# Index loads at the start, thin products in column groups, and the opening of the last stage of a four-layer graph network

## The chip, the cores and the metric

The kernel runs on one core of one Trainium2 chip. The metric is the device time of one launch in microseconds (us). Engines are named as in the profile: PE is TensorE's matmul, PEld its weight load, DVE is VectorE, ACT is ScalarE, POOL is GpSimd, SP is SyncE, which here only issues DMAs.

## The reference

512 nodes with 768 features pass through four layers. Each layer adds three things to the residual stream `x`: a graph network over 8704 directed edges, a linear attention ("mix"), and a feed-forward part. What matters for the change:

- The graph networks need, for each pair of nodes, how many edges of each type run between them, and for the first layer the sum of edge features per target node.
- Layers 1 (RGAT, two convolutions) and 3 (GAT) compute attention coefficients per node and head from thin products: 768 features against 24, 6 or 24 columns.
- The feed-forward parts of layers 0 and 2 are mixtures of 8 experts; a router product (768 by 8) picks one expert for each node.
- The last feed-forward part scores all nodes for 16 experts; each expert takes its 64 best nodes, and a shared expert takes all:

```python
sc = sigmoid(xn @ gate.T)                    # 512 x 16
for e in range(16):                          # expert e takes the 64 nodes of highest sc[:, e]
    h = silu(xn[top] @ Wg[e].T) * (xn[top] @ Wu[e].T)      # hidden width 3072
    out[top] += sc[top, e] * (h @ Wd[e].T)
out += (silu(xn @ Ws_g.T) * (xn @ Ws_u.T)) @ Ws_d.T        # hidden width 1536
```

All numbers are float32 on the outside; the kernel computes most products in float32, and the edge counts and a few exactly split operands in bfloat16.

## The kernel before, in words

The residual `x` stays on chip as four tiles of 128 nodes by 768. `xnT` is a normalized copy with features on partitions: six chunks of 128 features by 512 nodes. Every product accumulates over these six chunks in one PSUM tile of 128 by 512 (`ps`; eight exist). `acc` (L320) issues such a chain, `tr` (L325) a transpose, `copy` (L236, L238) empties PSUM on DVE and ACT by turns, `w` (L244) fetches a weight block of 1152 KB by an SP DMA into a ring of buffers. The engines' instruction orders are fixed when the program is built: a scheduler works through the program in its written order, with priorities, and an instruction waits only by semaphores. POOL, SP and ACT each have a queue of their own for the DMAs that they issue, and an issuing instruction takes its place in the engine's order.

**Start.** `Net.__init__` issues the loads of `x` (L179, 1.5 MB) and of the constant columns (L181) on POOL, then builds constants: identities, ones, iotas on POOL; `sel`, `identb`, `lower` and `number` on DVE. `counts` then loads four index vectors on POOL (L391), casts them (L392), builds edge weights `worth` (L399 to L401) and runs four passes, h and g each 0 and 1. A pass has 34 steps j; in each, DVE makes one-hot rows (`ohd` L465 in the first two passes, three `so` L468), and PE adds six 128x512 bf16 products to six PSUM tiles (L471), which an opening product with ones fills (L462). At the end of a pass the six tiles are copied out, split into digits (L478 to L485), and, in between, edge features of a quarter of the edges are split into three bf16 parts (L416 to L419) and multiplied (L424). The first layernorm and the first mix follow in the written order after the counts.

**Thin products.** The router products of both mixtures and of the last stage (`p[:E]` in `moe`, `p[:NX]` in `ffn3`), and the attention coefficients of `rgat` and the GAT, are chains of six matmuls with 8, 6, 16 or 24 stationary columns and 512 moving ones. The result has its few rows on partitions; four transposes turn it to nodes on partitions.

**Last stage.** `last_two` runs the last attention and the GAT side by side, and after the last projection normalizes the four tiles into `xn`; each is also written to DRAM (`there`, L1531, on ACT's queue). `ffn3` opens a ring of 10 weight buffers, transposes `xn` to `xnT`, computes the scores `sc` (Sigmoid, L1675), and ranks the nodes for each expert: `rank` transposes a broadcast of the scores, so that every node sees all others on its row, and DVE counts, per tile of 128 nodes, the greater ones before, the greater ones after, and equal ones with smaller index (L1687, L1690). `choose` compares ranks with 0..63 and gives a one-hot `oh`. For the first pair of experts `gather` multiplies `xn` by `oh` on PE (48 matmuls); for the seven later pairs `fetch` works out the row numbers and reads the rows from `there` by an indirect DMA of POOL (L1726), and `turn` transposes them. Then 64 steps of one 384-wide slice of two experts follow: `up` (L1794, two 64-column groups side by side), Silu, `down` (L1810). The slices of the shared expert, ranks and fetches of later pairs are spread between the steps by a table (`beside`). SP issues the weight blocks in the order of use, each as soon as its ring buffer is free.

Of the kernel before, what the change touches and what calls it, by code (L numbers as in the profile page):

```python
# [10 lines left out]
F32 = mybir.dt.float32  # L11
# [63 lines left out]

def _layout(i):
# [32 lines left out]
    for f, n, g in (("f0", "L0_ffn", "Ws"), ("f2", "L2_ffn", "Wg")):  # L109
        col(f + "_wg", _thin(i[f"{n}_{g}"]))  # L110
        a[f + "_w1"] = np.stack([_blocks(w)[0, 0] for w in i[n + "_W1"]])
        a[f + "_w2"] = _rows(i[n + "_W2"])
        a[f + "_b2"] = np.ascontiguousarray(i[n + "_b2"])
        col(f + "_b1", _col(i[n + "_b1"]))
# [31 lines left out]
    col("f3_gw", _thin(i["L3_ffn_gate_weight"].T))  # L146
# [18 lines left out]
class Net:  # L165
    def __init__(self, ctx, tc, dram, at, out):
# [11 lines left out]
        self.x = keep.tile([P, NT, D], F32, name="x")  # L178
        nc.gpsimd.dma_start(self.x, dram["x"].rearrange("(t p) d -> p t d", p=P))  # L179
        self.cols = keep.tile([P, dram["cols"].shape[1]], F32, name="cols")  # L180
# [6 lines left out]
        for i in range(3):  # L187
            nc.vector.tensor_copy(self.sel[32 * i : 32 * i + 32, :], self.ident[:32, :32])
        self.bias3 = self.rowp.tile([96, 2, D], BF16, name="bias3", bufs=1)
        nc.gpsimd.memset(self.bias3, 0.0)  # L190
        self.which = 0
        self.ones = keep.tile([P, P], F32, name="ones")
# [12 lines left out]
        nc.vector.tensor_copy(self.identb, self.ident)  # L205
        self.big0 = keep.tile([P, 1], F32, name="big0")
        nc.gpsimd.memset(self.big0, -BIG)
        self.onesb = keep.tile([P, P], BF16, name="onesb")
        nc.gpsimd.memset(self.onesb, 1.0)
# [3 lines left out]
        with tc.tile_pool(name="init", bufs=1) as ip:  # L213
            io = ip.tile([P, P], F32, name="io")
            nc.gpsimd.iota(io, pattern=[[1, P]], base=0, channel_multiplier=0, allow_small_or_imprecise_dtypes=True)
            nc.vector.tensor_scalar(self.lower, io, self.me, None, OP.is_gt)

        self.number = keep.tile([P, NT, 2], BF16, name="number")
        nc.vector.tensor_copy(self.number[:, :, 0], self.me.to_broadcast([P, NT]))
        for t in range(NT):  # L220
            nc.gpsimd.memset(self.number[:, t, 1:2], float(t * P))

# [95 lines left out]
    def acc(self, out, pairs):  # L318
        for n, (a, b) in enumerate(pairs):
            self.nc.tensor.matmul(out, a, b, start=n == 0, stop=n == len(pairs) - 1)  # L320
# [6 lines left out]
    def to_fm(self, x, out):  # L327

        ps = [self.ps() for _ in range(KC)]
# [22 lines left out]
    def norm1(self, x, out, t):  # L352
# [8 lines left out]
        nc.scalar.activation(r, mv[:, 1:2], AF.Sqrt, bias=self.eps)  # L361
# [9 lines left out]
    def counts(self, c0, g0):  # L371
# [10 lines left out]
        with ExitStack() as c:  # L382
# [7 lines left out]
            for n, a in enumerate(("src", "dst", "edge_type_3", "edge_type_4")):  # L390
                nc.gpsimd.dma_start(raw[:, n, :], d[a].rearrange("(p j) -> p j", p=P))  # L391
# [10 lines left out]
            io = one.tile([P, N], I16, name="io")  # L402
            nc.gpsimd.iota(io, pattern=[[1, N]], base=0, channel_multiplier=0)
# [6 lines left out]
            def features(q):  # L410
# [7 lines left out]
                nc.scalar.copy(part[:, 1], ea)  # L418
# [38 lines left out]
            for h in range(2):  # L457
                digit = {}
                for g in range(2):
# [3 lines left out]
                    for j in range(g * HJ, (g + 1) * HJ):  # L463
# [3 lines left out]
                        for n in range(3):  # L467
                            nc.vector.tensor_scalar(so[:, n, :], io[:, h * 256 : (h + 1) * 256], ind[:, 0, j : j + 1],  # L468
# [4 lines left out]
                    for (t, n), p in acc.items():  # L473
# [12 lines left out]
                        if g == 1:  # L486
                            finish(h, t, n, lo, hi, *digit[t, n])

                    for q in range((2 * h + g) * EJ // 8, (2 * h + g + 1) * EJ // 8):
                        features(q)  # L490
# [199 lines left out]
    def moe(self, f, act, xn, bs=None):  # L690
# [5 lines left out]
        with ExitStack() as c:  # L696
            one = c.enter_context(tc.tile_pool(name=f + "_one", bufs=1))
            two = c.enter_context(tc.tile_pool(name=f + "_two", bufs=2))
            xnT = one.tile([P, KC, N], F32, name="xnT")
# [8 lines left out]
            wg = self.col(f + "_wg", 0, KC * E).rearrange("p (k e) -> p k e", k=KC)  # L708
            p = self.ps()
            self.acc(p[:E], [(wg[:, k, :], xs[k]) for k in range(KC)])  # L710
            loT = one.tile([E, N], F32, name="loT")
            if bs is None:
                nc.vector.tensor_copy(loT, p[:E])
            else:
                nc.vector.tensor_scalar(loT, p[:E], self.col(bs, 0, 1, E), None, OP.add)
            p = self.ps()
            for t in range(NT):
                self.tr(p[:, t * E : (t + 1) * E], loT[:, t * P : (t + 1) * P])
            lo = one.tile([P, NT, E], F32, name="lo")
            nc.vector.tensor_copy(lo, p[:, : NT * E].rearrange("p (t e) -> p t e", t=NT))  # L720
# [423 lines left out]
    def fold(self, wq, l, H):  # L1144
# [19 lines left out]
        def turn(V, vt):  # L1164
            for a in range(2):
# [3 lines left out]
                nc.scalar.copy(V[:, 3 * a : 3 * a + 3],  # L1169
# [4 lines left out]
    def rgat(self, xT, l, H, V, C, done, between=None):  # L1174
# [4 lines left out]
        with ExitStack() as c:  # L1179
# [6 lines left out]
            qkT = one.tile([J, N], F32, name="qkT")  # L1186
# [8 lines left out]
            p = self.ps()  # L1195
            self.acc(p[:J], [(V[:, k].rearrange("p r h -> p (r h)"), xT[:, k, :]) for k in range(KC)])
            nc.scalar.copy(qkT, p[:J])
# [4 lines left out]
            def side():  # L1202
                p = self.ps()
                for t in range(NT):
                    self.tr(p[:, t * J : (t + 1) * J], qkT[:, t * P : (t + 1) * P])
                nc.scalar.copy(qk.rearrange("p t r h -> p (t r h)"), p[:, : NT * J])
                self.parts(qk3, qkT, qkT, mid, self.copies, nc.vector.tensor_sub)
# [60 lines left out]
    def gnn1(self, V1, xnT):  # L1268
        nc, tc, d = self.nc, self.tc, self.d
        with ExitStack() as c:  # L1270
# [34 lines left out]
            V2 = one.tile([P, KC, 3, 2], F32, name="V2")  # L1305
# [163 lines left out]
    def last_two(self, xn, xnT, out):  # L1469
# [5 lines left out]
        with ExitStack() as c:  # L1475
# [42 lines left out]
            for t in range(NT):  # L1518
# [8 lines left out]
                if over:  # L1527
                    while len(ready) <= t:
                        u = len(ready)
                        self.norm1(self.x, out, u)  # L1530
                        nc.scalar.dma_start(there[u * P : (u + 1) * P, :], out[:, u, :])  # L1531
# [4 lines left out]
    def fold3(self, one):  # L1536
# [7 lines left out]
        V = one.tile([P, KC, 2 * H], F32, name="V")  # L1544
# [10 lines left out]
    def gnn3(self, c, xnT, V):  # L1555
# [19 lines left out]
        qkT = one.tile([2 * H, N], F32, name="qkT")  # L1575
# [5 lines left out]
        p = self.ps()  # L1581
        self.acc(p[: 2 * H], [(V[:, k, :], xnT[:, k, :]) for k in range(KC)])
        nc.scalar.copy(qkT, p[: 2 * H])
        for t in range(NT):
# [7 lines left out]
            if t == 0:  # L1592
                q = self.ps()
                for u in range(NT):
                    self.tr(q[:, u * 2 * H : (u + 1) * 2 * H], qkT[:, u * P : (u + 1) * P])
                nc.scalar.copy(qk.rearrange("p t r h -> p (t r h)"), q[:, : NT * 2 * H])
                self.parts(qk3, qkT, qkT, mid, self.copies, nc.vector.tensor_sub)
# [42 lines left out]
    def ffn3(self, xn, xnT, there):  # L1640
# [5 lines left out]
        with ExitStack() as c:  # L1646
            one = c.enter_context(tc.tile_pool(name="f3_one", bufs=1))
            two = c.enter_context(tc.tile_pool(name="f3_two", bufs=2))
# [3 lines left out]
            self.wp = c.enter_context(tc.tile_pool(name="f3_w", bufs=10, side="right"))  # L1652

            first = self.small.tile([P, 1], F32, name="r3")
            nc.scalar.activation(first, self.eps, AF.Sigmoid)
            io = one.tile([P, P], F32, name="io")
            nc.gpsimd.iota(io, pattern=[[1, P]], base=0, channel_multiplier=0, allow_small_or_imprecise_dtypes=True)
            number = one.tile([P, NT, 2], F32, name="number")
            nc.gpsimd.tensor_copy(number, self.number)
# [5 lines left out]
            self.to_fm(xn, xnT)  # L1665
            gw = self.col("f3_gw", 0, KC * NX).rearrange("p (k e) -> p k e", k=KC)
            p = self.ps()
            self.acc(p[:NX], [(gw[:, k, :], xnT[:, k, :]) for k in range(KC)])
            loT = one.tile([NX, N], F32, name="loT")
            nc.vector.tensor_copy(loT, p[:NX])  # L1670
            p = self.ps()
            for t in range(NT):
                self.tr(p[:, t * NX : (t + 1) * NX], loT[:, t * P : (t + 1) * P])
            sc = one.tile([P, NT, NX], F32, name="sc")
            nc.scalar.activation(sc, p[:, : NT * NX].rearrange("p (t e) -> p t e", t=NT), AF.Sigmoid)  # L1675

            def rank(e):
# [4 lines left out]
                for t in range(NT):  # L1682
                    s = sc[:, t, e : e + 1]
                    for n, (a, b, op) in enumerate(((0, t * P, OP.is_ge), (t * P, N, OP.is_gt))):
                        if a < b:
                            junk = one.tile([P, N], F32, name="junk")
# [263 lines left out]
```

## Time and profile before

| what | before |
|---|---|
| time, median of 3 runs | 4281.39 us (4278.18 to 4281.85) |
| time of the profiled execution | 4283.03 us |
| its span, first to last instruction | 4281.2 us |
| mean granted clock of TensorE | 0.988 |
| PE / DVE / ACT / POOL busy | 4117.0 / 1299.7 / 659.5 / 268.9 us |
| moved by DMA | 710.30 MB |
| weight blocks by SP, last stage (Wg, Wu, Wd) | 3 x 128 of 1152 KB |

The span is cut into windows and slices; the busy time of an engine in a window says how full it was, "GB/s" what the DMA moved. PE runs nearly everywhere; its matmuls are pipelined, so that one row's duration (some 0.6 us) is longer than the distance of two starts (0.43 us for a float32 pass of 512 columns; each float32 matmul shows as two passes).

### The profile page before, as it was taken

The numbers are of one execution on the slowest core, as the hardware profiler recorded it, in microseconds if no ns is written. First come the engines' busy times: TensorE is split into PE (matmuls) and PEld (weight loads), VectorE is DVE, ScalarE is ACT, GpSimd is POOL, SyncE is SP. The second block draws the span as 40 slices with busy tenths as digits, with TensorE's granted clock in tenths as the row PEclk, the third lists the DMA queues.
The fourth block names the chain that finished last, engine by engine and source line by source line (L and its number), as shares of the span: only waits on it lengthen the run. The fifth ranks groups of instructions, "written<-read, shape, count | busy, mean of one in ns | idle before, by whom it ended". The sixth has DMA issues, their size and how long they took to land. (4 is left out here: it accounts for less than half of the span.)

```text
span 4281.2 us, 40171 instructions
## 1 busy us (share of the span) xinstructions
PE 4117.0 (96%) x16392; PEld 2100.7 (49%) x16392; DVE 1299.7 (30%) x3120; ACT 659.5 (15%) x1241; POOL 268.9 (6%) x316
## 2 busy tenths in 40 slices
PE   7989999999989999999999999989999999999998
PEld 3434555554445566755644444445654444444443
DVE  7772111112432125513220101035841122122211
ACT  2121200001312223411200000022610000000000
POOL 1120000001022010000000000021100000000000
PEclk9999999999999999999999999989999999999999
DMA  3111011111047112211201111063079999999998
GB/s 111 52 61 57 23 45 66 67 56 53 18 169 293 38 60 72 107 45 55 106 34 67 45 55 56 0 261 136 1 288 420 419 420 420 420 417 420 419 421 363
DMA packets 98955, 710.30 MB, mean 166 GB/s; under 512 B 12032, under 2 KB 12096, under 8 KB 29392
## 3 DMA queue, kind: packets, MB, share of 16 engines
q1 hardware_dynamic: 77776, 601.13, 35.3%
q0 software_dynamic: 16512, 93.97, 5.8%
q10 hardware_dynamic: 4480, 12.58, 0.8%
q8 instruction: 132, 2.16, 0.2%
q14 instruction: 55, 0.45, 0.0%
HBM read 685.09 MB, written 22.54 MB: 165 GB/s over the span
## 5 line engine op out<-in xcount | busy, mean ns | idle before, releaser
L1794 PE MATMUL ps<-w,xg 128*64 128x384 f32 x3072 | 566.0, 489 | 5.0 <-DMA w<-in_f_Wg_dram 3.0
L1794 PEld LDWEIGHTS ps<-w,xg 128*64 128x64 f32 x3072 | 234.1, 137 | 297.2 <-issue 271.0
L1427 PE MATMUL ps<-aT,w 128*128 128x512 f32 x864 | 372.3, 592 | 0.0
L1810 PE MATMUL ps<-w,hT 128*64 128x384 f32 x1536 | 321.0, 490 | 6.3 <-ACT hT L238 2.5
L320 PE MATMUL ps<-xnT,w 128*128 128x512 f32 (+1 forms) x732 | 320.3, 594 | 0.3 <-ACT xnT L238 0.2
L1427 PEld LDWEIGHTS ps<-aT,w 128*128 128x128 f32 x864 | 164.2, 190 | 203.6 <-issue 202.3
L320 PE MATMUL ps<-w,xnT 128*128 128x384 f32 x672 | 221.6, 486 | 0.2 <-DVE xnT L236 0.2
L320 PEld LDWEIGHTS ps<-xnT,w 128*128 128x128 f32 (+1 forms) x732 | 133.7, 184 | 174.7 <-issue 171.3
L1810 PEld LDWEIGHTS ps<-w,hT 128*64 128x64 f32 x1536 | 132.1, 136 | 169.1 <-issue 143.9
L368 DVE TENSOR_TENSOR x<-x,ps 128x384 f32<-128x384 f32 x224 | 123.4, 553 | 295.0 <-PE ps L320 223.6
L320 PE MATMUL ps<-C,parts 128*128 128x512 bf16 x864 | 189.8, 381 | 4.0 <-DVE inv L1449 4.0
L320 PE MATMUL ps<-w,hT 128*128 128x384 f32 x552 | 184.7, 490 | 3.9 <-ACTq L895 3.9
L471 PE MATMUL ps<-ohd,so 128*128 128x512 bf16 x816 | 181.9, 383 | 2.8 <-DVE so L468 2.8
L320 PEld LDWEIGHTS ps<-w,xnT 128*128 128x128 f32 x672 | 127.0, 190 | 88.6 <-issue 4.7
L1437 DVE TENSOR_TENSOR aT<-inv,ps 128x512 f32<-128x512 f32 x72 | 49.5, 688 | 367.2 <-PE ps L320 367.2
L1797 ACT ACTIVATE h<-ps 128x384 f32<-128x384 f32 x64 | 31.4, 491 | 794.8 <-PE ps L1794 794.8
L1798 DVE TENSOR_TENSOR h<-h,ps 128x384 f32<-128x384 f32 x64 | 35.5, 554 | 377.6 <-PE ps L1794 377.6
L320 PEld LDWEIGHTS ps<-w,hT 128*128 128x128 f32 x552 | 103.1, 190 | 81.4 <-ACT xbT L238 7.6
L320 PE MATMUL ps<-w,aT 128*128 128x384 f32 (+1 forms) x416 | 139.6, 486 | 0.5 <-DVE aT L236 0.4
L320 PEld LDWEIGHTS <-parts 128*128 128x128 bf16 x864 | 84.9, 98 | 110.0 <-issue 11.0
L320 PE MATMUL ps<-xnT,sw 128*128 128x512 f32 x288 | 138.3, 611 | 0.0
L468 DVE TENSOR_SCALAR so<-io,ind,worth 128x256 bf16<-128x256 int16 x408 | 121.7, 355 | 35.5 <-PE ps L471 35.4
(499 smaller groups left out, 4804.4 us busy)
## 6 DMA issues: line engine op xcount, KB each, us to landing
w<-in_f_Wg_dram SPq DMA_DIRECT2D x128, 1152.0 KB, 14.5
w<-in_f_Wu_dram SPq DMA_DIRECT2D x128, 1152.0 KB, 15.2
w<-in_f_Wd_dram SPq DMA_DIRECT2D x128, 1152.0 KB, 16.0
w<-in_g_w_dram SPq DMA_DIRECT2D x54, 1152.0 KB, 5.1
w<-in_m_wqkv_dram SPq DMA_DIRECT2D x24, 1152.0 KB, 6.6
w<-in_g_t_dram SPq DMA_DIRECT2D x12, 1152.0 KB, 5.8
w<-in_m_wp_dram SPq DMA_DIRECT2D x8, 1152.0 KB, 5.3
ea<-in_edge_attr_dram SPq DMA_DIRECT2D x34, 256.0 KB, 2.7
```

The lines of the kernel that those rows point to most:

```text
L320: self.nc.tensor.matmul(out, a, b, start=n == 0, stop=n == len(pairs) - 1)
L368: self.nc.vector.tensor_add(xs, xs, p)
L468: nc.vector.tensor_scalar(so[:, n, :], io[:, h * 256 : (h + 1) * 256], ind[:, 0, j : j + 1], worth[:, n, j : j + 1], OP.is_equal, OP.mult)
L471: nc.tensor.matmul(p, so[:, n, t * P : (t + 1) * P], ohd[:, j, :], start=False, stop=j == (g + 1) * HJ - 1)
L1427: nc.tensor.matmul(outs[nb * 3 + f], w[:, k, f * P : (f + 1) * P], xT[:, k, :], start=first and k == 0, stop=last and k == KC - 1)
L1437: nc.vector.tensor_mul(aT[:, f, :], inv[:, r, :], p)
L1794: nc.tensor.matmul(p[a * 64 : a * 64 + 64, :HW], xg[:, k, a * CAP : (a + 1) * CAP], ws[b][a][:, k, :], start=k == 0, stop=k == KC - 1)
L1797: nc.scalar.activation(h, pg[:, :HW], AF.Silu)
L1798: nc.vector.tensor_mul(h, h, pu[:, :HW])
L1810: nc.tensor.matmul(po[nb][a * 64 : a * 64 + 64, :HW], hT[:, f * P + a * 64 : f * P + a * 64 + 64], wd[a][:, f, nb * HW : (nb + 1) * HW], s ...
```

## The change

Three things are edited. **Start:** the index loads move from POOL's queue to those of SP and ACT, ahead of everything else there; `onesb` and the iota become POOL's first work; DVE's constants go to a function `constants`, which together with the first layernorm is issued after the last `so` (and the last feature part) of the third pass; the first pass's features are issued after the third `so`. **Narrow groups:** `narrow` computes the thin products with weights padded to 32 columns, chunk k in columns 32*(k%4), so that the PSUM tile holds four partial sums; these are added by products with `fours`, four identities of 32 on top of each other (`narrow_tm` gives nodes on partitions; in `rgat` and the GAT a further product gives heads on partitions). The router weights get loads of their own. **Last stage:** `to_fm` can copy the first three node tiles before the last is there, `xn` is given up after it and its room taken by a ring of 13 weight buffers, `there` is written from POOL's queue, Sigmoid's table is called for after the last square root, the first two ranks are computed half by ACT's Sign with a sum, half by a DVE compare with a sum, and the first pair's nodes are fetched from DRAM as the others are, with a second product of the shared expert put between.

The order on each engine in the new program: DVE begins with the cast of the indices; SP with two index loads, then the edge features; ACT with the other two. In the ranks, Sign and the DVE compare of one tile alternate on the two engines, each waiting for the other's read of the shared PSUM tile.

```diff
+        self.onesb = keep.tile([P, P], BF16, name="onesb")
+        nc.gpsimd.memset(self.onesb, 1.0)
+        self.io = keep.tile([P, N], I16, name="io")
+        nc.gpsimd.iota(self.io, pattern=[[1, N]], base=0, channel_multiplier=0)
         nc.gpsimd.dma_start(self.x, dram["x"].rearrange("(t p) d -> p t d", p=P))
...
+        self.fours = keep.tile([P, 32], F32, name="fours")
+        for i in range(4):
+            nc.gpsimd.tensor_copy(self.fours[32 * i : 32 * i + 32, :], self.ident[32 * i : 32 * i + 32, 32 * i : 32 * i + 32])
...
+    def constants(self):
+        nc = self.nc
+        for i in range(3):
+            nc.vector.tensor_copy(self.sel[32 * i : 32 * i + 32, :], self.ident[:32, :32])
+        nc.vector.tensor_copy(self.identb, self.ident)
+        nc.vector.tensor_scalar(self.lower, self.io[:, :P], self.me, None, OP.is_gt)
+        nc.vector.tensor_copy(self.number[:, :, 0], self.me.to_broadcast([P, NT]))
...
+    def narrow(self, w, xs):
+        p = self.ps()
+        for k in range(KC):
+            g = 32 * (k % 4)
+            self.nc.tensor.matmul(p[g : g + 32], w[:, k, :], xs[k], start=k < 4, stop=k + 4 >= KC)
+        return p
+
+    def narrow_tm(self, four, n):
+        p = self.ps()
+        for t in range(NT):
+            self.acc(p[:, t * n : (t + 1) * n], [(four[:, t * P : (t + 1) * P], self.fours[:, :n])])
+        return p[:, : NT * n].rearrange("p (t n) -> p t n", t=NT)
...
-                nc.gpsimd.dma_start(raw[:, n, :], d[a].rearrange("(p j) -> p j", p=P))
+                (nc.sync, nc.scalar)[n % 2].dma_start(raw[:, n, :], d[a].rearrange("(p j) -> p j", p=P))
...
+                    if h == 1 and g == 0:
+                        self.begun = made["so"].ins, made["part"].ins
                     for q in range((2 * h + g) * EJ // 8, (2 * h + g + 1) * EJ // 8):
-                        features(q)
+                        if h == g == 0:
+                            with tc.issue_after(made["third"]):
+                                features(q)
+                        else:
+                            features(q)
...
-                net.norm(net.x, xn)
+                with tc.issue_after(net.begun[0]), tc.issue_after(net.begun[1]):
+                    net.constants()
+                    net.norm(net.x, xn)
...
+            wg = one.tile([P, KC, 32], F32, name="wg")
+            nc.scalar.dma_start(wg.rearrange("p k e -> p (k e)"), d[f + "_wg"])
...
-            self.acc(p[:E], [(wg[:, k, :], xs[k]) for k in range(KC)])
-            loT = one.tile([E, N], F32, name="loT")
+            p = self.narrow(wg, xs)
+            loT = one.tile([P, N], F32, name="loT")
...
-            for t in range(NT):
-                self.tr(p[:, t * E : (t + 1) * E], loT[:, t * P : (t + 1) * P])
-            nc.vector.tensor_copy(lo, p[:, : NT * E].rearrange("p (t e) -> p t e", t=NT))
+            nc.vector.tensor_copy(lo, self.narrow_tm(loT, E))
...
+                self.acc(p[:J], [(self.fours[:, :J], qkT)])
+                nc.scalar.copy(qk.rearrange("p t r h -> p t (r h)"), self.narrow_tm(qkT, J))
+                self.parts(qk3, p[:J], qkT[:J], mid, self.copies, nc.vector.tensor_sub)
...
-                        nc.scalar.dma_start(there[u * P : (u + 1) * P, :], out[:, u, :])
+                        nc.gpsimd.dma_start(there[u * P : (u + 1) * P, :], out[:, u, :])
...
-            self.wp = c.enter_context(tc.tile_pool(name="f3_w", bufs=10, side="right"))
+            self.wp = c.enter_context(tc.tile_pool(name="f3_w", bufs=13))
...
+            side = one.tile([P, 7 * P], BF16, name="side")
+            nc.gpsimd.memset(side[:, : 3 * P], 0.5)
+            nc.gpsimd.memset(side[:, 4 * P :], -0.5)
+            nc.gpsimd.tensor_scalar(side[:, 3 * P : 4 * P], before, -0.5, None, OP.add)
...
+            BIGGER = 2.0 ** 60
+            nc.vector.tensor_scalar(low, sc[:, :, :2], -BIGGER, None, OP.mult)
...
+            def first_rank(e):
+                p = self.ps()
+                for t in range(NT):
+                    self.tr(p[:, t * P : (t + 1) * P], sc[:, t, e : e + 1].to_broadcast([P, P]))
+                for t in range(NT):
+                    junk = one.tile([P, N], BF16, name="sign")
+                    i = nc.scalar.activation(junk, p, AF.Sign, scale=BIGGER, bias=low[:, t, e : e + 1],
+                                             accum_out=signs[:, t, e : e + 1])
+                    junk = one.tile([P, N], BF16, name="junk")
+                    nc.vector.scalar_tensor_tensor(junk, p, sc[:, t, e : e + 1], side[:, (3 - t) * P : (7 - t) * P],
+                                                   OP.is_equal, OP.mult, accum_out=sides[:, t, e : e + 1])
+                return i
...
-            rest = pieces[1:]
+            rest = pieces[2:]
...
             for e in range(2):
-                rank(e)
-            shared(0, 0)
+                last = first_rank(e)
+            nc.vector.tensor_scalar(signs, signs, 0.5, float(N // 2), OP.mult, OP.add)
+            nc.vector.tensor_add(above[:, :, :2], signs, sides)
+            with tc.issue_after(last.ins):
+                last = shared(0, 0)
             choose(0)
-            gather(0)
+            with tc.issue_after(last.ins):
+                last = fetch(0)
+            with tc.issue_after(last.ins):
+                shared(0, 1)
+            turn(0)
             held = up(*steps[0], up_w(*steps[0]))
```

`oh`, `junk` and `number` are bf16 now, and the tiles `rows` and `os` have one buffer each in place of two.

## The prediction

> **What bounds the kernel now.** I read the page's rows in slices first, then the table of windows, then the waits of TensorE (PE), then the timeline where these disagree. TensorE is busy 96% of the span, so a microsecond counts only where it empties TensorE, or where something else is the limit.
>
> ```profile
> PE 4117.0 (96%) x16392; PEld 2100.7 (49%) x16392; DVE 1299.7 (30%) x3120; ACT 659.5 (15%) x1241; POOL 268.9 (6%) x316
> PE   7989999999989999999999999989999999999998
> GB/s 111 52 61 57 23 45 66 67 56 53 18 169 293 38 60 72 107 45 55 106 34 67 45 55 56 0 261 136 1 288 420 419 420 420 420 417 420 419 421 363
> ```
>
> Two ends show themselves: the first slice is only 7 tenths full, and from slice 30 on (3200 us) the DMA stands at 420 GB/s without a gap. The windows of the last stage (time, then PE, PE's weight loads, DVE, ACT, POOL, then clock, DMA share, GB/s) say which is the limit there:
>
> ```profile
> 3140.00:3150.00 10.00, 7.50 (x26) 2.88 (x25) 2.62 (x8) 2.11 (x4) 0.00 (x0) 0.94 1.02 418
> 3160.00:3170.00 10.00, 9.41 (x58) 8.61 (x60) 2.26 (x7) 0.48 (x1) 0.00 (x0) 0.71 0.78 323
> 3170.00:3180.00 10.00, 10.00 (x54) 4.51 (x51) 3.13 (x12) 0.49 (x1) 0.00 (x0) 1.00 0.64 238
> 3180.00:3190.00 10.00, 10.00 (x54) 4.10 (x52) 3.26 (x14) 0.49 (x1) 0.55 (x1) 1.00 0.90 363
> 3500.00:3700.00 200.00, 199.38 (x990) 87.93 (x987) 38.17 (x100) 11.61 (x23) 4.79 (x8) 1.00 1.01 420
> ```
>
> In 3500 to 3700 PE looks full, but its up-products (L1794) sum to 566.0 us over 64 groups, where one undisturbed group took 7.96: 64 x 7.96 = 509. The 57 us between are matmuls held inside a group by weights. So the weight stream sets the end of the last stage. Its only losses are the dips at 3160 to 3190, and its start.
>
> The start is the longest wait of TensorE (us in total, times, longest), and the timeline tells its cause (start, duration, and in brackets the idle time before and its releaser):
>
> ```profile
> PE ps L424 <- DVE ohd L465: 17.1, 1, 17.1
> 5.99 0.57 POOL L391 DMA_DIRECT2D so<-in_src_dram  x1
> 16.43 1.48 DVE L359 BATCH_NORM_STATS2 st<-x 128x6 f32<-128x384 f32 x3 [9.39 <-DMA x<-in_x_dram]
> 24.34 0.27 DVE L392 CAST ind<-so 128x272 f32<-128x272 int32 x1
> 26.42 1.06 PE L471 MATMUL ps<-ohd,so 128*128 128x512 bf16 x2
> ```
>
> The indices are issued on POOL behind x and the constants, and DVE casts them only after the layernorm of x, for which it sat idle 9.39 us.
>
> **Start: -17.5 us.** The indices become the first DMAs of SP and ACT, so they are issued at about 0.7 to 1.9. The nearest row is ea's DMA on SP, issued at 0.73 and there for its reader at 3.62, so the last index should land near 4. From the cast to the first so is 25.58 - 24.34 = 1.24, to the first count matmul 0.84 more: 4 + 0.3 + 1.0 gives 5.3 to 5.6 instead of 26.42, or -21. TensorE's opening L462 (2.73 us, now ready by 1.5 because onesb is POOL's first work) is done before that. ea on SP slips by two issues, 0.9 us; its features are put behind the third so and DVE ran 1.04 us per j (0.77 + 0.27) against TensorE's 1.295, so their 2.8 us of DVE work are hidden in about 11 j.
>
> The layernorm and constants are not gone. DVE had for them, from 16.43 to 24.34, 8.8 us of work; four square roots and two table loads (1.28 each) on ACT go along. They now stand behind the last so of the third count pass, in front of the copies that empty its accumulators (216 to 244 before). There DVE had about 7 us idle between the features, and TensorE lost 2.4 (waits of 0.35, 0.31, 1.26, 0.49 at the pass's end). The cover is those 7 us and the 38 feature matmuls (8.37 us) that TensorE does meanwhile. Bounds: all but 1 us hidden, or all 8.8 late at L462, which waits for emptied accumulators. The idle time lies partly later than the copies, and TensorE has its own feature matmuls meanwhile, so I take 3.5. Sum -21 + 3.5 = -17.5, from -20 to -12.
>
> **Narrow groups: -10.7 us.** A thin product costs as much as a full one:
>
> ```profile
> 1225.88 1.89 DVE L236 COPY xnT<-ps 128x512 f32<-128x512 f32 x3 [0.42 <-PE ps L325]
> 1226.62 5.32 PE L320 MATMUL ps<-xnT,cols 128*8 128x512 f32 x12 [0.24 <-DVE xnT L236]
> 1231.98 0.74 DVE L715 TENSOR_SCALAR loT<-ps,cols 8x512 f32<-8x512 f32 x1 [4.22 <-PE ps L320]
> ```
>
> Twelve passes at 0.43. The kernel already has one product in 32-column groups, mix0's half times sq (L555): its first passes start at 394.760, 394.766 and 394.773, the second ones at 395.213 to 395.226. So groups share a pass of 0.44; six chunks as four plus two need 4 x 0.44 = 1.76 instead of 5.16. The Trainium skill, TensorEngine Tiling (Array Packing), Key Properties, speaks against it: a change of tiling mode drains the engine. By the rule each switch costs a full pass end (0.59 lasting, 0.43 spaced: 0.16; ten switches 1.6 us). The row has 0.523 from the wide pass to the first group instead of 0.43, and 0.521 on the way out: 0.09, ten switches 0.9 us. I take the row.
>
> The four partial sums must be added: four small f32 products against stacked identities take the place of four transposes (0.41). The near row is number times oh, eight such pairs in 0.95; so +0.54. In the RGAT layers and the GAT one 128x512 f32 product (2 x 0.43) is added.
> - f0 and f2: the copies of xnT end 1.89 after their start, so the last two chunks wait until 1227.8; the end falls at about 1228.9 instead of 1231.95: -3.1 + 0.54 + 0.18 = -2.4 each.
> - two RGAT layers: -3.4 + 0.87 + 0.5 = -2.0 each.
> - GAT: -1.9, its last chunks wait for copies a little.
> Sum -10.7. The layers are full of TensorE work, so it counts whole. If groups did not overlap in these chains it would be +4 (added products alone); if only in pairs, -4. Best case -13. The extra copying over 128 rows instead of 8 costs nothing: a copy is paid by its 512 columns.
>
> **Last stage: -7.3 us.** Time zero is the end of the last projection, 3135.7; the first Wg DMA waits for it in both kernels. Against 420 GB/s the stream lost in 3160 to 3170 97 x 10 / 420 = 2.3, then 4.3, 1.4 and 0.2 (411 in the next ten): 8.2 us. With 10 buffers it runs dry until the first up-products release one:
>
> ```profile
> 3160.15 0.90 DVE L1701 TENSOR_TENSOR oh<-io,above 128x128 f32<-128x128 f32 x4
> 3160.59 8.07 PE L320 MATMUL ps<-oh,xn 128*128 128x128 f32 x48 [4.76 <-DVE oh L1701]
> 3168.59 7.96 PE L1794 MATMUL ps<-w,xg 128*64 128x384 f32 x48
> 3172.70 0.81 SPq L244 DMA_DIRECT2D w<-in_f_Wg_dram  x2
> 3208.48 1.04 POOL L1726 DMA_INDIRECT rows<-f_there,who  x1 [25.34 <-DMA w<-in_f_Wd_dram]
> ```
>
> Thirteen blocks of 1.18 MB last 13 x 2.81 = 36.5 us, so until about zero + 38. The first release (Wg) comes 4.1 after the first up; up must begin by zero + 33.5. Its chain: ranks begin at zero + 9 instead of 13.0 (the cut to_fm and narrow product save 3.4, the sigmoid's table load 1.28). The ranks themselves do not get faster: eight Signs on ACT, each 0.59 and 0.10 to read its sum, and eight DVE steps of 0.75 and 0.08 read the same PSUM tile and wait for one another in the program's order, 8 x (0.69 + 0.05 + 0.77 + 0.05) - 0.7 = 11.7 against 11.4 (3148.72 to 3160.12). Then above, oh, who: +2.4, to 23.1. The gather (8.07 us on TensorE) becomes a fetch from DRAM: row 3208.48 had its packets in by 3215.66, 7.2 later, under the same full stream; so zero + 30.3, turn and copy 1.0, up at 31.3 (32.9 before). The shared product with Wu, 5.3 us, lies beside the fetch. The fetch's wait for the DRAM copies of xn (now on POOL's queue, last one issued at about zero + 3.5, 8.7 to land as on ACT's: 12.2) ends earlier; what stands behind it on POOL are the shared weights' loads, not needed before 45. So the dips go, and 0.39 MB of rows are added (+0.9): -7.3. Bounds -9 and, with up later than 33.5 by three, -4.
>
> **Sum.** -17.5 - 10.7 - 7.3 = -35.5 on the profiled execution's 4283.03 us (span 4281.2, 1.8 around it): 4247.5; from the median of 4281.39: 4246.
>
> **Rivals.**
> - The last stage keeps its dips (0.13): a second stall, such as the loads of POOL's queue before the rows' fetch, puts up near zero + 40. Against it: the release order above. 4246 + 7 = 4253.
> - The narrow groups run one behind the other (0.12). For it: in L555 all groups have one weight, here each chunk has its own, to be loaded; against: L1794's 64-column pairs do it 64 times (0.164 per pass instead of 0.323). 4246 + 13 = 4259.
> - The constants cost all 8.8 (0.12): 4251.
> - Slower (0.02): the clock. It was granted 0.988 in the mean, but 0.71 in 3160 to 3170 behind a half-idle TensorE. If the new gaps, or denser counts, lower it in the 3135 us before the stream, each 0.01 costs 31 us; it decides from a mean of 0.976 on there, and at 0.970 it gives 4300. For it: the counts have windows of 0.84 and 0.73 already. Against: 500 to 1000 and 1500 to 2500 ran at 1.00 with fuller work.
> - The change does not do what it says: sign ranks no faster than before, as worked out. That is in the sum at nothing.
>
> **How the numbers follow.** The forecast (0.59) is 4246; two of the rivals together (0.02) give about 4262. The range: best ends -20 - 13 - 9 = -42 give 4239, a little more if the start's copies hide everything and the stream gains its ramp: 4234. The rivals reach 4259, two together the upper end. Within 0.2% is 8.6 us, about what a measurement can tell from no change: it takes a clock of 0.98 or the like, 0.02 with slower; slower 0.02; faster 0.96.
>
> **What would show it.** First count matmul near 5.4; a wait of some microseconds at L462 in the transition near 200; narrow products of some 1.8 to 2.3 us; DMA share 1.0 from 3140's counterpart on without a dip; Sign and is_equal alternating over 11 to 12 us; first up near zero + 31. Wrong if the first counts wait for x still, if the narrow product's passes stand 0.43 apart, or if the stream dips again before the first release.

## The result: 46 us less, of which the last stage gave half

The changed kernel takes 4235.4 us (median of 4, 4234.7 to 4237.6) against 4281.6 (median of 4): a ratio of 0.9892, with a 95% interval of 0.9876 to 0.9908. The forecast was 4246, in a range from 4234 to some 4262, so the gain of 46.2 us was a third larger than the 35.5 foretold. The changed kernel was not measured again beside its variants below. The kernel before was, and its median lay between 4280.5 and 4281.6 each time, so a difference of 1 or 2 us between variants is not told by the times alone.

The profiled execution has a span of 4233.6, 47.6 less. Two marks that both programs pass cut it into three parts: the product of `over` with ones, which ends the counts, and the first transpose of `xn` behind the last projection. First the kernel before, then the changed one (start, duration):

```profile
317.47 0.16 PE L320 MATMUL ps<-over,onesb 128*128 128x4 bf16 x1 [1.52 <-DVE over L492]
3135.68 2.13 PE L325 MATMUL ps<-ident,xn 128*128 128x128 f32 x18
```

```profile
304.23 0.16 PE L333 MATMUL ps<-over,onesb 128*128 128x4 bf16 x1 [1.52 <-DVE over L542]
3111.24 2.13 PE L354 MATMUL ps<-ident,xn 128*128 128x128 f32 x18
```

| part | measured | forecast |
|---|---|---|
| start to end of counts | 304.23 - 317.47 = -13.2 | -17.5 |
| layers up to the last projection | -24.4 + 13.2 = -11.2 | -10.7 |
| last stage | -47.6 + 24.4 = -23.2 | -7.3 |

So the layers came out as worked out, the start gave less, and the last stage three times as much. The changed kernel's windows of the last stage, and the page's row of the stream's speed:

```profile
GB/s 111 53 64 56 23 45 67 68 56 54 18 178 291 42 56 72 109 45 56 98 44 57 55 56 53 4 237 155 12 282 427 427 427 426 427 427 427 420 425 366
```

```profile
3140.00:3150.00 10.00, 9.18 (x53) 4.05 (x53) 1.25 (x2) 0.97 (x2) 0.56 (x1) 1.00 1.02 430
3160.00:3170.00 10.00, 9.26 (x53) 4.45 (x50) 2.63 (x8) 0.00 (x0) 0.00 (x0) 1.00 1.02 430
3500.00:3700.00 200.00, 199.38 (x1034) 89.24 (x1030) 43.54 (x124) 12.37 (x25) 4.24 (x7) 1.00 1.01 427
```

The dips (323, 238 and 363 GB/s before) are gone, as forecast. What was not: the stream runs at 427 GB/s where it had 420, at the same DMA share of 1.01. Over the stage's 453 MB of weights (384 blocks) that alone would be 453/0.420 - 453/0.427 = 17.7 us. The first up-products begin 32.2 after the last projection (forecast 31.3, before 32.9), when the fetched rows have been turned:

```profile
3120.37 0.69 ACT L1735 ACTIVATE sign<-ps,low 128x512 bf16<-128x512 f32 x1 [0.74 <-PE ps L354]
...
3121.26 0.75 DVE L1738 SCALAR_TENSOR_TENSOR junk<-ps,sc,side 128x512 bf16<-128x512 f32 x1 [1.43 <-ACT sign L1735]
...
3122.05 0.69 ACT L1735 ACTIVATE sign<-ps,low 128x512 bf16<-128x512 f32 x1 [0.91 <-DVE junk L1738]
...
3135.00 1.04 POOL L1781 DMA_INDIRECT rows<-f_there,who  x1 [8.23 <-DVE who L1779]
...
3142.25 0.88 PE L354 MATMUL ps<-ident,rows 128*128 128x128 f32 x6 [0.50 <-DMA rows<-f_there,who]
3143.44 7.96 PE L1851 MATMUL ps<-w,xg 128*64 128x384 f32 x48 [0.32 <-DVE xg L249]
```

Sign and compare alternate, each waiting for the other, from 3120.37 to 3132.4: 12.0 us, against 11.7 worked out.

### The profile page after: what moved, and what is told of

Read it like the earlier page. It is cut to its first block, busy times and chain, and to the rows that moved or that the text cites. A ratio compares the mean times of both kernels' runs of the same rounds, so it can differ in the third digit from the quotient of the medians.

```text
span 4233.6 us, 40102 instructions
## 1 busy us (share of the span) xinstructions
PE 4092.9 (97%) x16356; PEld 2094.4 (49%) x16356; DVE 1295.3 (31%) x3096; ACT 664.4 (16%) x1258; POOL 274.2 (6%) x325
## 5 line engine op out<-in xcount | busy, mean ns | idle before, releaser
L514 PEld LDWEIGHTS <-so 128*128 128x128 bf16 x816 | 79.7, 99 | 107.6 <-DVE so L511 14.3
```

The source lines that it names most:

```text
L514: nc.tensor.matmul(p, so[:, n, t * P : (t + 1) * P], ohd[:, j, :], start=False, stop=j == (g + 1) * HJ - 1)
```

## Experiments on the weight stream

The packet records show how the stream became faster. A packet of 9216 bytes (one partition of a weight block) takes 0.351 us in the median before, one in ten 0.358 or more; in the changed kernel nearly all take 0.347. The memory map of the two builds differs in where the ring lies: before at the upper end, first byte 137184, that is 480 above a multiple of 512; after at the lower end, 108544, a multiple of 512 (a buffer of 9216 bytes is 18 times 512, so all buffers share the remainder). Theory A is that this start address sets the stream's speed, and through it much of the last stage's gain; its rival stands in the expectations below, quoted as written before each run.

**Shifted ring in the changed kernel.**

```diff
+            shift = c.enter_context(tc.tile_pool(name="f3_pad", bufs=1)).tile([P, 120], F32, name="f3_pad")
+            nc.gpsimd.memset(shift, 0.0)
             self.wp = c.enter_context(tc.tile_pool(name="f3_w", bufs=13))
```

> The changed kernel with its ring of 13 buffers moved up by 480 bytes in every partition, so that a buffer begins at 480 above a multiple of 512 as in the kernel before (there 137184, here 109024). Theory A, the start address sets the speed of the weight stream: a packet of 9216 bytes takes 0.351 us again, the stream falls from 427 to about 420 GB/s, and the time rises by some 15 us to about 4250. Theory B, more buffers or the other work of the stage make the stream faster: 427 GB/s and 4235 us as before the shift.

4247.8 us, 12.4 more; 421 GB/s, packets of 0.351 and 0.358 again. Where the time goes can be read in TensorE's timeline of the shifted kernel: 1058 us after the last projection it is 1.9 us behind the changed kernel, at the last matmul 13.3. So nearly all is lost in the last 60 us, where the weights come late.

```profile
3500.00:3700.00 200.00, 199.38 (x1033) 89.34 (x1030) 43.53 (x125) 12.46 (x25) 4.24 (x7) 1.00 1.01 421
```

```profile
4193.37 3.12 PE L1869 MATMUL ps<-w,hT 128*64 128x384 f32 x17 [0.84 <-DMA w<-in_f_Wd_dram]
4198.97 4.09 PE L1853 MATMUL ps<-w,xg 128*64 128x384 f32 x24 [1.51 <-DMA w<-in_f_Wg_dram]
4204.55 3.76 PE L1853 MATMUL ps<-w,xg 128*64 128x384 f32 x21 [1.02 <-DMA w<-in_f_Wu_dram]
4210.15 3.12 PE L1869 MATMUL ps<-w,hT 128*64 128x384 f32 x17 [0.86 <-DMA w<-in_f_Wd_dram]
```

The changed kernel has no such wait at its end (0.1 us of idle TensorE in its last 55, against 8.6). From 3500 to 3700 both do the same number of matmuls within one (1033, 1034): TensorE runs at its own pace out of the ring's stock, and pays when the stock and the work beside the steps are used up. Theory A holds here. That the pad's own presence is not the cause shows in the next run, where the packets are short behind the same pad.

**Aligned ring in the kernel before.** The same pad of 480 bytes, on the upper side, moves its ten buffers down to multiples of 512.

> The kernel before with its ring of 10 buffers moved down by 480 bytes, so that each buffer begins at a multiple of 512. Theory A (start address): packets of 0.347 us, 427 GB/s, and 15 to 17 us less, about 4265. Theory B (number of buffers, other side of the memory): 420 GB/s and no change, 4281.

4278.1 (20 runs) against 4280.9 (24 runs), ratio 0.9995, interval 0.9988 to 1.0002: 3 us in the medians, not told from none, and not 15. In the profiled executions the last stage is 4.4 us shorter. Its packets do take 0.347, but the stream does not run faster:

```profile
3170.00:3180.00 10.00, 10.00 (x50) 4.57 (x47) 3.96 (x16) 0.49 (x1) 0.00 (x0) 1.00 0.73 275
3500.00:3700.00 200.00, 199.38 (x986) 87.87 (x983) 38.16 (x100) 11.61 (x23) 4.78 (x8) 1.00 1.00 420
```

The share falls to 1.00 and the dip at 3170 stays. Between 3200 and 4200, SP waits 856 us for TensorE's products to give a buffer back, and 0.3 for transfers. TensorE has more to do here than in the changed kernel. So neither theory was right for this kernel: the packets answer to the address, and something else is equally near.

**Less work for TensorE in the kernel before.**

```diff
-                oh = two.tile([P, NT, 2, CAP], F32, name="oh")
+                oh = two.tile([P, NT, 2, CAP], BF16 if q else F32, name="ohb" if q else "oh", bufs=2 if q else 1)
...
-                self.acc(p[:, :2], [(oh[:, t].rearrange("p e s -> p (e s)"), number[:, t, :]) for t in range(NT)])
+                self.acc(p[:, :2], [(oh[:, t].rearrange("p e s -> p (e s)"), self.number[:, t, :]) for t in range(NT)])
```

> The kernel before with one small piece of the change: the one-hot oh of the seven later pairs, and the numbers that it is multiplied with, in bf16 (the first pair keeps float32 for its gather; the ring stays at 10 buffers and at its old start address). The products of oh with the row numbers shrink from 5.7 to some 0.7 us in all. Theory of the prediction, the weight stream sets the end of the last stage: no change, 4281. Rival, TensorE sets the pace until the last steps: each microsecond taken off TensorE there counts, -5 or, if the stream at the end takes some of it back, -2 to -4: 4276 to 4279.

4280.5 against 4280.5, ratio 1.000 (0.9991 to 1.0009, or 4 us to either side, so the time alone does not exclude the rival's 2 to 4). The trace decides. The products did shrink, from 5.7 to 0.7 us counted from the start of each to the start of the next. But the up-products grew by 2.7 and the down-products by 2.0 when counted in this way, so 4.7 of the 5.0 came back. Part of it are waits for weights in the last steps (4225 to 4280), which grew from 7.3 to 8.6 us. As the prediction had it, the stream takes back what TensorE gains in the kernel before.

**Both together.**

> The kernel before with both: its ring moved down by 480 bytes to multiples of 512 (alone 4278.1 against 4280.9) and oh in bf16 for the seven later pairs (alone 4280.5 against 4280.5). Theory C, in the kernel before the weight stream and TensorE's own work end within about 3 us of each other, so that each gain alone is hidden by the other: together 6 to 9 us less, 4272 to 4275. If one of the two alone were the bound, the sum of the single effects, -3, 4278.

4272.0 against 4280.5, ratio 0.9981 (0.9974 to 0.9988): -8.5, where the single effects sum to -3, which lies outside the interval (-11 to -5). In the profiled executions the last stage is shorter by 10.1, against 4.4 and 1.1 for the two alone. Each gain was hidden by the other bound. TensorE's work and the stream end within a few microseconds of one another in the kernel before, and a change has to shorten both.

**Ring of ten in the changed kernel** (13 becomes 10, same start address).

> The changed kernel with 10 ring buffers in place of 13, at the same start address. Theory A (start address): 427 GB/s stays once the stream runs; only the dip before the first up-products returns, 10 blocks at 2.76 us are 28 us and the first buffer comes free at 36, so 6 to 8 us more, about 4242. Theory B (number of buffers makes the stream faster): 420 GB/s through the stage, 4257 or so.

4241.8 (4235.9 to 4244.0), 6.4 more, as theory A had it. The dip is back, once, and the stream has 427 later:

```profile
3140.00:3150.00 10.00, 8.14 (x50) 3.71 (x50) 1.24 (x2) 0.97 (x2) 0.56 (x1) 1.00 0.58 215
3500.00:3700.00 200.00, 199.38 (x1034) 89.37 (x1030) 43.53 (x124) 12.43 (x25) 4.24 (x7) 1.00 1.01 427
```

The dip's loss is (427 - 215) x 10 / 427 = 5.0 us of the 6.4.

**Ring shifted by 64 bytes** (16 floats in place of 120).

> The changed kernel with its ring moved up by 64 bytes. If a start at a multiple of 64 bytes is enough for short packets: 0.347 us, 427 GB/s, 4235. If a larger unit counts (the Trainium skill's page DMA: Bandwidth & Descriptors, on how a descriptor splits, has 256 bytes): packets of 0.351 to 0.358 us as with the shift by 480, 421 GB/s, 4248.

4244.8, 9.4 more than unshifted: 422 GB/s, packets of 0.349 in the median and 0.356 at the slow end. A multiple of 64 is not enough. In its direction this fits what the Trainium skill says (DMA: Bandwidth & Descriptors, How a descriptor splits into AXI transactions): a transfer is cut at multiples of 256 bytes, and one that starts between them begins with a piece from the boundary below. An estimate from this is 37 in place of 36 pieces here, 2.8%. The size does not fit: between 3500 and 3700 us the mean packet grew from 0.3474 to 0.3527 us with the shift by 480, 1.5%, and to 0.3512 with the shift by 64, 1.1%. The page speaks of bytes that are fetched, while here the place written to was moved. No run here tells 256 from 128 or 512, so the mechanism stays open.

## Experiments on the ranks

**First ranks on VectorE alone** (`rank` in place of `first_rank`).

> The changed kernel with the first two ranks counted by VectorE alone, as before the change, in place of Sign on ScalarE beside a compare on VectorE. By the prediction, ranks of 11.7 us with signs against 11.4 without: the first up-products begin at the same place within 1 us, 4235. If the signs helped by the 4 to 5 us that half the work would be worth: 4237 to 4240.

4236.2 (4229.4 to 4242.9), first up-product 32.0 after the last projection against 32.2: the signs are worth nothing, as forecast.

**Two PSUM tiles.**

```diff
-                p = self.ps()
-                for t in range(NT):
-                    self.tr(p[:, t * P : (t + 1) * P], sc[:, t, e : e + 1].to_broadcast([P, P]))
+                p, p2 = self.ps(), self.ps()
+                for b in (p, p2):
+                    for t in range(NT):
+                        self.tr(b[:, t * P : (t + 1) * P], sc[:, t, e : e + 1].to_broadcast([P, P]))
...
-                    nc.vector.scalar_tensor_tensor(junk, p, sc[:, t, e : e + 1], side[:, (3 - t) * P : (7 - t) * P],
+                    nc.vector.scalar_tensor_tensor(junk, p2, sc[:, t, e : e + 1], side[:, (3 - t) * P : (7 - t) * P],
```

> The changed kernel with the scores of each of the first two experts transposed twice, into one PSUM tile for ScalarE's Sign and another for VectorE's compare, so that the two need not alternate. The ranks should take some 6.5 us in place of 12, and the first up-products begin 5 to 6 us earlier, at 26 to 27 after the last projection. If TensorE sets the pace and the ring's stock holds, -5 us: 4230. If the weight stream is what counts at the end, less than 2: 4234, with waits for weights in the last steps.

The ranks take 7.2 us and no longer alternate:

```profile
3120.18 0.69 ACT L1736 ACTIVATE sign<-ps,low 128x512 bf16<-128x512 f32 x1 [0.74 <-PE ps L354]
...
3120.70 0.75 DVE L1739 SCALAR_TENSOR_TENSOR junk<-ps,sc,side 128x512 bf16<-128x512 f32 x1 [1.05 <-PE ps L354]
...
3121.00 0.69 ACT L1736 ACTIVATE sign<-ps,low 128x512 bf16<-128x512 f32 x1
...
3121.50 0.75 DVE L1739 SCALAR_TENSOR_TENSOR junk<-ps,sc,side 128x512 bf16<-128x512 f32 x1
```

The time is 4233.4, only 2.0 less; the profiled last stage is 1.8 shorter. The first up-product comes only 3.7 earlier (28.5 after the last projection), because the fetched rows, asked for 5 us earlier, are there 8.3 us after POOL's issue where it was 7.2. TensorE now stands idle for 4.1 us before them:

```profile
3138.23 1.28 PE L354 MATMUL ps<-ident,rows 128*128 128x128 f32 x6 [4.10 <-DMA rows<-f_there,who]
3139.52 9.12 PE L1852 MATMUL ps<-w,xg 128*64 128x384 f32 x48
```

```profile
3140.00:3142.00 2.00, 2.00 (x8) 0.71 (x6) 0.00 (x0) 0.03 (x1) 0.00 (x0) 0.52 1.02 432
```

Of the 3.7, 2.0 are lost again by the end. The first group of up-products takes 9.12 us where the changed kernel's takes 7.96, and the granted clock was 0.52 in that window, where the changed kernel has 1.00 from 3140 on. That is 1.2 us; the other 0.8 are lost within the next 130 us, for a reason that stays open. So the time lies between the two expectations, but the waits for weights in the last steps are not seen: after the first up-product TensorE's list of waits names no weight block.

## Experiments on the start and the thin products

**The start alone, in the kernel before.** The diff is the start part of the change.

> The kernel before with the edit of the start alone (index loads on SP and ACT, onesb and iota first, constants and layernorm after the third pass's last so, first features after the third so). Theory of the prediction: -17.5, 4264. From the trace of the changed kernel, where the counts end 13 us earlier: -13, about 4268, with the stretch from 12 to 18 us slow on DVE while POOL splits the bias rows.

4266.4 against 4280.9, ratio 0.9965 (0.9951 to 0.9979): -14.5, between the two expectations and nearer the trace's. In its own trace the counts end 12.8 us earlier.

**POOL's element work behind the counts, in the changed kernel.** `mix0`'s two bias rows, and likewise the copies into `fours`, are issued after the last DMA of `finish` on POOL.

```diff
+                self.poolq = nc.gpsimd.dma_start(self.S32[2 * h + t], S).ins
...
+            with tc.issue_after(self.poolq):
+                bv = self.bias(d["m0_bv"])
```

> The changed kernel with POOL's element work at the start put behind the counts: the split of two bias rows (12.8 to 18 us in the trace of the changed kernel) and the four copies of identities (4.9 to 5.9). Theory: DVE's one-hot steps were slow there (0.94 us in place of 0.27) because POOL worked at the same time, which cost TensorE some 5 us; the count matmuls then run at 1.295 us per step from the start, and the time falls by 4 to 6, to 4230. Rival: DVE was slow for another reason (the DMAs of x and the weights, which run in the same microseconds): no change.

4229.3 (4228.9 to 4230.2), 6.1 less; the counts end 6.0 earlier. In the changed kernel VectorE's three `ohd` from 13.71 on take 2.81 us and the three `so` behind them 2.23, while POOL splits bias rows. Without POOL's work, below, three of either kind take 0.87 and 0.85. First the changed kernel, VectorE and then POOL:

```profile
12.43 1.37 DVE L511 TENSOR_SCALAR so<-io,ind,worth 128x256 bf16<-128x256 int16 x3 [0.62 <-PE ps L514]
13.71 2.81 DVE L506 TENSOR_SCALAR ohd<-io,ind 128x512 bf16<-128x512 int16 x3
16.45 2.23 DVE L511 TENSOR_SCALAR so<-io,ind,worth 128x256 bf16<-128x256 int16 x3
```

```profile
13.79 1.75 POOL L291 TENSOR_TENSOR row<-row,bias 1x768 f32<-1x768 f32 x1
15.51 0.87 POOL L290 CAST bias<-row 1x768 bf16<-1x768 f32 x1
16.45 1.63 POOL L291 TENSOR_TENSOR row<-row,bias 1x768 f32<-1x768 f32 x1
```

And with POOL's work put later:

```profile
12.39 0.86 DVE L512 TENSOR_SCALAR so<-io,ind,worth 128x256 bf16<-128x256 int16 x3 [0.54 <-PE ps L515]
13.17 0.87 DVE L507 TENSOR_SCALAR ohd<-io,ind 128x512 bf16<-128x512 int16 x3
13.96 0.85 DVE L512 TENSOR_SCALAR so<-io,ind,worth 128x256 bf16<-128x256 int16 x3
```

One by one, the four slow VectorE steps from 12.95 on took 0.85, 1.72, 0.91 and 1.72 us, and each ended within 0.2 us of the POOL instruction beside it (0.90, 1.75, 0.87 and 1.63); a step between them took 0.34. The DMAs of x and the weights run at 416 and 415 GB/s in the two kernels (window 10 to 25), so they are not the cause. That agrees with the Trainium skill (SBUF — State Buffer, Who interferes with whom): a VectorE instruction in a mode that uses two ports shares the second pair with GpSimd, and the one that comes second is held for the whole instruction. No run here shows in which mode these steps ran.

**Narrow groups undone, in the changed kernel.** `narrow` becomes one chain, `narrow_tm` four transposes, the extra products go.

```diff
-        for k in range(KC):
-            g = 32 * (k % 4)
-            self.nc.tensor.matmul(p[g : g + 32], w[:, k, :], xs[k], start=k < 4, stop=k + 4 >= KC)
+        self.acc(p[:32], [(w[:, k, :], xs[k]) for k in range(KC)])
...
-            self.acc(p[:, t * n : (t + 1) * n], [(four[:, t * P : (t + 1) * P], self.fours[:, :n])])
+            self.tr(p[:, t * n : (t + 1) * n], four[:n, t * P : (t + 1) * P])
```

> The changed kernel with the narrow groups undone: each thin product is again one chain of six float32 matmuls into one group of 32 columns, followed by four transposes; everything else stays. By the prediction's sum for this part 10.7 us slower, by the traces (11.2 between the end of the counts and the last projection) 11 slower plus up to 3 in the last stage, where the product stands before the first ranks: 4246 to 4249.

4249.0 (4246.2 to 4250.7), 13.6 more, as expected with the share of the last stage (in the traces 11.7 up to the last projection and 2.7 behind it). One product in the changed kernel: the copies pace it, 2.25 us instead of 5.32, and the sum of the four parts comes after.

```profile
1213.47 2.25 PE L341 MATMUL ps<-xnT,wg 128*32 128x512 f32 x12 [0.24 <-DVE xnT L249]
1215.80 0.75 DVE L765 TENSOR_SCALAR loT<-ps,cols 128x512 f32<-128x512 f32 x1 [1.18 <-PE ps L341]
1216.60 1.06 PE L333 MATMUL ps<-fours,loT 128*128 128x8 f32 x8 [0.88 <-DVE loT L765]
```

**Both improvements together.**

> The changed kernel with both improvements that the experiments gave: POOL's element work at the start put behind the counts (alone -6.1) and two PSUM tiles for the first ranks (alone -2.0). They lie in different stages, so their gains should add: 4227.5, below both kernels.

4228.4 (4227.0 to 4231.1), ratio 0.9879 (0.9864 to 0.9894): below both kernels. The time is not told from POOL's part alone (4229.3). The traces show the second gain: from the last projection to the last matmul it took 1116.5 us, against 1118.4 with POOL's part alone, about the 1.8 of the run with two PSUM tiles.

## Why the prediction was right, and where its sizes were off

The total came out inside the range with errors of both signs. The start gave 4.3 less than forecast, the layers 0.5 more, the last stage 15.9 more. With the start address undone (the shifted ring) the change gives 4247.8, 1.8 beside the forecast; that closeness is in part luck, since there too 4.3 missing at the start stand against 2.5 more in the last stage.

- **Start, first count matmul: right in kind, 1.7 late.** It stands at 7.07, not 5.3 to 5.6. The indices landed as estimated (cast at 4.05), but from the cast to the first `so` it took 2.5 us, not 1.24. First the kernel before, then the changed one:

```profile
24.34 0.27 DVE L392 CAST ind<-so 128x272 f32<-128x272 int32 x1
25.58 0.34 DVE L468 TENSOR_SCALAR so<-io,ind,worth 128x256 bf16<-128x256 int16 x1
25.84 0.22 DVE L401 TENSOR_TENSOR worth<-worth,so 128x68 f32<-128x68 f32 x1
```

```profile
3.10 1.41 POOL L198 MEMSET bias<- 96x1536 bf16 x1
4.05 0.61 DVE L434 CAST ind<-so 128x272 f32<-128x272 int32 x1 [2.67 <-DMA so<-in_edge_type_dram]
6.12 0.23 DVE L443 TENSOR_TENSOR worth<-worth,so 128x68 f32<-128x68 f32 x1
6.55 0.84 DVE L511 TENSOR_SCALAR so<-io,ind,worth 128x256 bf16<-128x256 int16 x3
```

  The kernel before finishes one of the three parts of `worth`, starts the one-hot steps, and adds the other two parts between them. The changed kernel finishes all three first, from 5.39 to 6.35: that is 0.9 of the 1.3 us. The other 0.3 is the cast. It ends at 4.66 or 4.67 in three runs (changed kernel, POOL's work later, start alone), though it begins at 4.05, 3.83 and 3.67, each time just behind POOL's memset, which ends at 4.5. That the memset held it is likely and was not tested. The copies into `fours` are not the cause: with them put later the first `so` still stands at 6.59.
- **Start, DVE hides the rest: wrong.** "DVE ran 1.04 us per j" was taken from 25 to 60 us, where POOL is idle. In the kernel before, POOL had split the bias rows ahead of the counts; now the counts run beside that work. The lead of 19.3 us at the first count matmul had shrunk to 14.4 at the 51st. The experiment with POOL's work moved gives 6.1 us back.
- **Start, 3.5 us given back in the transition: did not happen.** The counts stand at -12.86 before the transition and -12.91 behind it. The constants' rows sum to 1.2 us of DVE there, not 3.7 as before: `sel` 0.53 instead of 1.74 and `identb` 0.23 instead of 1.57. In the kernel before, POOL's split of the bias rows ran beside them (18.80 to 23.81). The 8.8 us for layernorm and constants was also too large as a reading: it adds rows that overlap, in the 7.9 us from 16.43 to 24.34. The two errors of the start partly cancel.
- **Narrow groups: right.** -11.2 measured between the marks, 13.6 by undoing, of which the last stage's own product is a part. The switch out of a group shows the 0.52 us from start to start that was read from the row before (1576.27 to 1576.79), not the full pass end.
- **The last stage is bounded by the stream: right, but only just.** The bf16 run shows it. The argument from 566 us of busy time does not: rows of matmuls overlap, so the 57 us "held inside a group by weights" were not there. In the changed kernel, where TensorE's list of waits names no weight block, the same row is as long, and from start to start the up-products take 524.6 before and 527.4 after:

```profile
L1851 PE MATMUL ps<-w,xg 128*64 128x384 f32 x3072 | 567.1, 489 | 0.3 <-DVE xg L249 0.3
```

  TensorE was only a few microseconds behind as second bound, and the prediction did not see it.
- **-7.3 for the last stage: the term missing from the sum was the start address of the ring.** "The dips go" is what happened, and without the address the stage gains 1131.4 - 1141.2 = -9.8 (from the last projection to the last matmul, the shifted kernel against the one before); the address adds -13.3. Of the 9.8, three buffers more are worth about 6, if they are worth the same as with the aligned start (the ring of ten); the stage's other edits were not run one by one. In the kernel before, the address alone is worth about 3 in the medians, and 8.5 together with 5.0 us of TensorE work taken off by bf16. The changed kernel has 5.3 more taken off, by the shared product put into the wait. Whether the address needs the thirteen buffers too was not run.
- **The ranks are not faster: right,** 12.0 us, and 4236.2 without signs.
- **Rivals:** the mean clock stayed (0.989 against 0.988); the groups overlap; the dips went; the constants cost nothing, less than the bound of 1 us set for them.

## What to carry to other kernels

Look at where a ring of DMA buffers begins before its depth is tuned: a change of side or of neighbours can move the address, and the speed of every transfer with it. Where the time doesn't answer to a faster engine or to a faster stream alone, try both at once before either is called free. Before a prologue is shortened, ask whether the engine behind it will stand idle: the first products after the idle time may run at a lower clock. Take the duration of a moved step from a row whose neighbours are like those it will have, GpSimd's above all.

## What the runs showed of the hardware

- A 9216-byte packet into on-chip memory took 0.347 us from a start at a multiple of 512 and mostly 0.349 to 0.358 from one at 64 or 480 above it; the stream ran at 427 against 420 to 422 GB/s.
- Three of VectorE's one-hot steps of 128x512 took 0.87 us without GpSimd's work and 2.81 beside its work on one partition.
- A float32 product in four groups of 32 columns took 1.91 us for six chunks of 512 columns, where one chain took 5.32.
- After 4.1 us of idle TensorE, with a granted clock of 0.52 in the window, 48 up-products took 9.12 us; at 1.00 they took 7.96.
